# Keeping four engines in the source's order in two stages of a three-layer Trainium2 kernel, and moving one logarithm

## The chip, the cores and the metric

The kernel runs on one core of a Trainium2 chip. The core has a matrix engine (TensorE, PE in the profile; its weight loads are PEld), a vector engine (VectorE, DVE), a scalar engine for table functions (ScalarE, ACT), a general engine (GpSimd, POOL), and a queue of transfers issued by SyncE (SP). Each engine has its own stream of instructions and works it off in order; between engines, semaphores make a consumer wait for its producer. The metric is the device time of one execution in microseconds. Beside the timed runs one execution is recorded by the hardware profiler.

## What is computed

Eight images of 32 x 32 pixels with 128 channels, in 32-bit floats, pass three layers, each of which adds its result to the image.

1. *Attention*: queries, keys and values from a normalised image, four heads of 32 channels, 1024 pixels by 1024 pixels.
2. *Mixer*: each image is a sequence of 1024 tokens, worked in both directions by a state-space layer.
3. *Spectral stage*: a convolution along the sequence with fixed filters.

The heart of the mixer, cut to what matters here (c are the 16 chunks of 64 tokens):

```python
zxbcdt = x @ in_proj
z, xbc, dt = split(zxbcdt)
xbc = silu(causal_conv(xbc, conv_w) + conv_b)      # 4 taps
xh, Bm, Cm = split(xbc)
dt = softplus(dt + dt_bias);  dA = dt * A
Acs = cumsum(dA within a chunk);  xdt = xh * dt
Y_diag = einsum(Cc, Bc, exp(segsum(dA)), xdt)
states = einsum(Bc, exp(Acs_last - Acs), xdt)      # one per chunk
prev   = scan(states, exp(Acs_last))               # state before each chunk
Y_off  = einsum(Cc, prev, exp(Acs))
yg = (Y_diag + Y_off + xh * D) * silu(z)
out = (yg * rsqrt(mean(yg * yg) + eps) * norm_w) @ out_proj
```

The softplus is built of an exponential, a logarithm and a few small operations.

## The kernel before, in words

The kernel is one program in which Python functions emit instructions. A builder then fixes the order of each engine's stream. Unless it is told otherwise, it may let a later instruction go ahead of an earlier one on the same engine where the data allow it; it puts in the semaphores that the chosen order needs. Tiles come from pools with a fixed number of buffers, and a new tile in a buffer waits for the last reader of the old one.

*Attention* (about 95 to 505 us) loops over 8 images, 2 halves of the queries and 8 tiles of keys. `scores` makes the products pt (PE, L480) and their exponential pr (ACT, L485); `weigh` multiplies by the values (PE, L500) and adds two key tiles (`two`, DVE, L509); `total` sums those over the keys (PE pd, L520); `project` takes the reciprocal of the sums in small pieces (den), applies it to av, and adds the projected result to the image X. The loop is written as a pipeline: scores of step n, sums of step n-2, weights of step n-1, and a piece of `project`.

*The mixer* (about 505 to 1190 us) loops over 16 units: sequence 0 direction 0, sequence 0 direction 1, sequence 1 direction 0 and so on. A unit's iteration finishes this unit and prepares the next one, `following`. If the next unit starts a new sequence (it is then called `fresh`; this is so in each unit of direction 1 but the last), the sequence's normalised tokens are turned and its step sizes made as well. The functions and the tiles they fill, in the source's order:

- `decays`: three small products in the tile misc (PE, L794), then their exponentials rest and dec (ACT, L796 and L800)
- `turn_x`: xs is transposed (sx, PE, L810) and multiplied by the step sizes (xdt, DVE, L813)
- `turn_sums` of the unit before: two transposes of its sums of squares, in misc (PE, L1015), then a reciprocal root (rms, POOL, L1019)
- `turn_b`: sb (PE, L827), from which bk is copied (ACT, L835)
- `decayed_x`: xdd (DVE, L842), from xdt and rest, and gm
- `add_up` of the unit before: its result into X (DVE, L1026)
- `turn_tokens`, if fresh: the normalised tokens b_x are transposed (px, PE, L656)
- `between`: pl (PE, L856) from dau, and its exponential lm (ACT, L863)
- `steps`, if fresh: a generator in three pieces. The first makes pd on PE, sp_v on DVE and an exponential on ACT; the second makes sp_u, its logarithm on ACT, and sp_u again; the third makes the step sizes dt, and da.
- `chunk_states`: pst (PE, L893), from bk and xdd
- `pass_states`: the chain over the chunks, 29 dependent steps on DVE (state, L907 and L910), and four transfers on SP's queue (moved)
- `from_start`: pe (PE, L873) from dau and its exponential ec (ACT, L880)
- `spread`, for the next unit: da spread out to dau on POOL (L710)
- `project_x` and `project_z`, for the next unit: pp and pz on PE, copied or activated by ACT to xp, xs and zs
- `weigh_decays`: lm times gm (DVE, L931) and ec times ct (DVE, L935)
- `outputs`: sy (PE, L959) from xdt, lm, state, moved and ec
- `convolve` (DVE, L749), `activate_x` (ACT, L754), `project_bc` (pb, PE, L769) and `activate_bc` (bt and ct, ACT, L785) for the next unit
- `gate`, two halves: y (DVE, L974 and L982) and its square (ACT)
- `normalize`, in units of direction 0: statistics of the next sequence (b_st and b_mv on DVE, a reciprocal root ln_r on POOL)
- `project_out`: spo (PE, L989); `square_sums`: misc (PE, L1001) and its copy sums (ACT, L1009)
- `normalized`, in units of direction 0: b_shift on DVE, and b_x in eight pieces on ACT (L647)

In PSUM two buffers rotate among sx, sb, px, pl, pd, pe, pp, pz and pb, and two among pst, sy, spo and misc. [...] the exponential, the logarithm and the silu used here need loads between them (ACT_TABLE_LOAD).

Before the change the order of all engines' streams in these loops is the builder's. In the trace of before one sees, for instance, that the first four sx stand ahead of the decays on PE, that lm's product runs ahead of the chain of states, and that b_x runs between the two exponentials of lm.

## Time and profile before

| | |
|---|---|
| three runs, median (lowest, highest) | 1656.2 us (1654.26, 1657.62) |
| profiled execution | 1658.12 us |
| its span, first to last instruction | 1656.0 us |
| mean granted TensorE clock | 0.963 |
| busy, PE | 1502.1 us (91% of the span) |
| busy, DVE | 1145.9 us (69%) |
| busy, ACT | 884.4 us (53%) |
| busy, POOL | 438.8 us (26%) |
| largest groups of the two stages | exponential pr 248.1, pt 162.5, two 159.9, po 149.0, convolution 117.7, pb 114.1, state 87.3 us |

Times are in microseconds. The page divides the span in 40 slices and gives a digit for each engine and slice, its busy share in tenths. Its list of groups gives for a line, an operation and a tile the busy time, the mean of one instruction, and what ended the idle time before it. A timeline row gives the start, the length, the engine, the line, the operation, the tile written and those read, the shapes, and how many instructions the row joins (x2); in brackets stands the idle time of the engine before the row and what ended it.

### The profile page before, as it was taken

Reading aid. Unit: us, or ns where it says so; the run is one execution under the profiler, and the core shown is the slowest. Engines: PE = TensorE matmul, PEld = TensorE weight load, DVE = VectorE, ACT = ScalarE, POOL = GpSimd, SP = SyncE. Lnnn points to the kernel's source line nnn. Section 1 sums busy time; section 2 is a strip of 40 time slices with the busy share of each in tenths; the row PEclk is TensorE's granted clock in tenths of the full one; section 3 lists DMA queues with packets and bytes.
Section 4 is the critical chain, followed back from the end, with each engine's and each line's share of the span. In section 5 each row is a group of like instructions: output and inputs, shape, how many; then the busy total and the mean of one; then the engine's idle time right before and its main releaser. Section 6 shows DMA issues by size and latency. Waiting matters only on the chain. (4 is left out here: it accounts for less than half of the span.)

```text
span 1656.0 us, 45655 instructions
## 1 busy us (share of the span) xinstructions
PE 1502.1 (91%) x20118; PEld 910.7 (55%) x20118; DVE 1145.9 (69%) x2211; ACT 884.4 (53%) x1205; POOL 438.8 (26%) x504
## 2 busy tenths in 40 slices
PE   4679999999997999999999999999587899999977
PEld 3442222223223566666665666665376888888863
DVE  6856767777676787787877787878444466666745
ACT  2326666666665565656565656565154255555530
POOL 6428888500001111111112111111065401001100
PEclk9899999999997999999999999999788899999998
DMA  5002212100000000000100000000258512223238
GB/s 147 0 1 62 66 50 61 39 1 1 1 1 0 14 14 26 14 26 14 27 13 26 14 26 13 26 14 26 72 169 214 158 48 74 67 61 80 70 101 313
DMA packets 131958, 89.03 MB, mean 54 GB/s; under 512 B 41480, under 2 KB 114824, under 8 KB 131752
## 3 DMA queue, kind: packets, MB, share of 16 engines
q1 hardware_dynamic: 129640, 81.84, 17.6%
q8 instruction: 160, 2.62, 0.7%
q10 hardware_dynamic: 2112, 4.19, 0.7%
q14 instruction: 46, 0.38, 0.1%
HBM read 44.60 MB, written 33.55 MB: 47 GB/s over the span
## 5 line engine op out<-in xcount | busy, mean ns | idle before, releaser
L485 ACT ACTIVATE pr<-pt 128x1024 f32<-128x1024 f32 x256 | 248.1, 1021 | 121.6 <-PE pt L480 94.3
L509 DVE TENSOR_TENSOR two<-pr,pr 128x1024 f32<-128x1024 f32 x128 | 159.9, 1280 | 98.0 <-PE pd L520 98.0
L1260 DVE COPY gs<-pg 128x512 f32<-128x512 f32 x256 | 164.8, 686 | 85.8 <-PE pg L1249 80.7
L1262 ACT COPY gs<-pg 128x512 f32<-128x512 f32 x256 | 138.7, 595 | 147.3 <-PE pg L1249 131.4
L480 PE MATMUL pt<-q,k 32*128 32x512 f32 x1024 | 162.5, 642 | 5.2 <-DVE taps L356 3.5
L1249 PE MATMUL pg<-taps,mst 32*128 32x128 f32 x4096 | 160.7, 287 | 6.8 <-ACT gs L1262 6.8
L1249 PEld LDWEIGHTS pg<-taps,mst 32*128 32x128 f32 x4096 | 136.4, 189 | 31.6 <-issue 17.1
L500 PE MATMUL po<-pr,v 128*32 128x512 f32 x1024 | 149.0, 603 | 0.0
L1283 PE MATMUL py<-gs,u 128*32 128x128 f32 (+1 forms) x4096 | 145.2, 282 | 0.7 <-ACT gs L1262 0.4
L1283 PEld LDWEIGHTS py<-gs,u 128*32 128x32 f32 (+1 forms) x4096 | 112.6, 144 | 16.0 <-issue 0.9
L749 DVE SCALAR_TENSOR_TENSOR xs<-xp,cw,xs 128x1024 f32<-128x1024 f32 x96 | 117.7, 1293 | 2.1 <-ACT xs L741 2.1
L813 DVE TENSOR_TENSOR xdt<-sx,dt 128x1024 f32<-128x1024 f32 x32 | 37.8, 1220 | 115.2 <-PE sx L810 115.2
L769 PE MATMUL pb<-bxt,wbc 128*128 128x512 f32 x256 | 114.1, 598 | 2.0 <-issue 1.1
L480 PEld LDWEIGHTS pt<-q,k 32*128 32x128 f32 x1024 | 55.3, 184 | 102.9 <-PE pt L480 40.2
L1019 POOL TENSOR_TENSOR rms<-rms_v,mhalf 128x8 f32<-128x8 f32 x16 | 39.2, 2447 | 224.8 <-DVE rms_v L1017 224.8
L1272 POOL TENSOR_SCALAR u<-u 128x512 f32<-128x512 f32 x16 | 23.9, 1492 | 249.2 <-DMA u<-ud 235.7
L710 POOL TENSOR_TENSOR dau<-upto,da 128x2048 f32<-128x2048 f32 x16 | 57.9, 3620 | 116.0 <-PE pe L873 94.2
L520 PE MATMUL pd<-two,ones 128*32 128x512 f32 x512 | 84.8, 605 | 3.6 <-DVE two L509 2.4
L910 DVE SCALAR_TENSOR_TENSOR state<-state,dec,pst 128x64 f32<-128x64 f32 x448 | 87.3, 275 | 0.9
L769 PEld LDWEIGHTS pb<-bxt,wbc 128*128 128x128 f32 x256 | 47.2, 189 | 57.4 <-issue 54.7
L500 PEld LDWEIGHTS po<-pr,v 128*32 128x32 f32 x1024 | 28.8, 109 | 88.2 <-issue 87.9
L959 PEld LDWEIGHTS sy<-lm,xdt 64*64 64x64 f32 x2048 | 63.1, 137 | 21.1 <-issue 20.4
(279 smaller groups left out, 2920.0 us busy)
## 6 DMA issues: line engine op xcount, KB each, us to landing
ud<-sp SPq DMA_DIRECT2D x8, 1024.0 KB
u<-ud SPq DMA_DIRECT2D x32, 256.0 KB
yd<-sums SPq DMA_DIRECT2D x32, 256.0 KB
moved<-state SPq DMA_DIRECT2D x48, 128.0 KB
yt<-yd SPq DMA_DIRECT2D x6, 1024.0 KB
X<-in_x SPq DMA_DIRECT2D x8, 512.0 KB
part_p<-in_L_ffn_M_phi_plus SPq DMA_DIRECT2D x32, 128.0 KB
part_m<-in_L_ffn_M_phi_minus SPq DMA_DIRECT2D x32, 128.0 KB
```

Of the source, the lines that this page charges most:

```text
L480: nc.tensor.matmul(pt[:, i, :], lhsT=k[rows, j * P : (j + 1) * P], rhs=q[rows, cols], start=True, stop=True)
L485: nc.scalar.activation(pr[:, 2 * g : 2 * g + 2, :].rearrange("p i t -> p (i t)"), pt.rearrange("p i t -> p (i t)"), AF.Exp,)
L500: nc.tensor.matmul(po[rows, :], lhsT=vs[b][:, j, rows], rhs=pr[:, h, :], start=(j == 0), stop=(j == NT - 1))
L509: nc.vector.tensor_tensor(two, sums["pr"][:, 2 * g : 2 * g + 2, :], pr[:, 2 * g : 2 * g + 2, :], ALU.add)
L520: nc.tensor.matmul(sums["d"][(2 * g + i) * DH : (2 * g + i + 1) * DH, :], lhsT=ones[:, :DH], rhs=two[:, i, :], start=(j == 1), stop=(j == ...
L749: nc.vector.scalar_tensor_tensor(acc, xp[:, at : at + T], cw[u.d][:, n, i : i + 1], acc, ALU.mult, ALU.add)
L769: nc.tensor.matmul(u.pb[:, i * 512 : (i + 1) * 512], lhsT=wbc[u.d][:, k, :], rhs=xt[:, at : at + 512], start=(k == 0), stop=(k == KC - 1),)
L910: nc.vector.scalar_tensor_tensor(u.state[:, k, h, :], u.state[:, k - 1, h, :], u.dec[:, c, j, h : h + 1], u.pst[c][:, j, h, :], ALU.mult, ...
L1249: nc.tensor.matmul(pts[g][:, e, :], lhsT=mst[rows, n * 4 + e, :], rhs=taps[rows, cols].rearrange("p f q m i -> p (f q m i)"), start=True, ...
L1260: nc.vector.tensor_copy(to, frm)
L1262: nc.scalar.copy(to, frm)
L1283: nc.tensor.matmul(py[t * 32 : t * 32 + 32 - 16 * m, q, :], lhsT=u[:, i, m:, :, :, q * FC + f].rearrange("p k b i -> p (k b i)"), rhs=mats ...
```

## The change

Two kinds of edit are made.

- Before the attention loop, and again before the mixer's loop over units, a section is opened in which PE, DVE, ACT and POOL keep the order in which the source emits their instructions. SP's queue is not in the set. Stages outside of the two sections stay the builder's.
- In the mixer's loop the second piece of `steps` (with the logarithm) no longer follows `chunk_states`; it comes after `from_start`, where the third piece stood. The third piece (dt and da) now comes after `project_x` of the next unit, and `project_x` comes ahead of `spread`.

```diff
+IN_ORDER = {
+    mybir.EngineType.PE,
+    mybir.EngineType.DVE,
+    mybir.EngineType.Activation,
+    mybir.EngineType.Pool,
+}
...
         prs, ending = {}, iter(())
+        s.enter_context(tc.manual_schedule(engines=IN_ORDER))
         for n in range(len(units) + 2):
             if n < len(units):
                 prs[n] = scores(*units[n])
...
         activate_bc(first)
 
+        s.enter_context(tc.manual_schedule(engines=IN_ORDER))
         last = None
         misc = wide_psum(ps_s, "misc")
...
                 going = steps(following.b, following.seq)
                 next(going)
             chunk_states(u)
-            next(going, None)
             pass_states(u)
             from_start(u)
             next(going, None)
             if following:
+                project_x(following)
+                next(going, None)
                 spread(following)
-                project_x(following)
                 project_z(following)
             weigh_decays(u)
             outputs(u)
```

No arithmetic is altered.

## The prediction

> **What bounds the kernel now.** I read the page's slices first (40 of 41.4 us each), to see where TensorE is the limit.

> ```profile
> PE   4679999999997999999999999999587899999977
> DVE  6856767777676787787877787878444466666745
> ACT  2326666666665565656565656565154255555530
> ```

> The columns are time. Slices 4 to 12 are attention, 13 to 28 the mixer: TensorE stands at 9 in both but for the seam, VectorE at 6 to 8, ScalarE at 5 or 6. So both stages run at TensorE's pace, and the change costs or saves only what it adds to or takes from TensorE's idle time. The page's chain of work is cut short at a few per cent of the span and says nothing on the mixer; I read TensorE's waits there, 540 to 1160 us, instead.

> ```profile
> engine line waited for: us in total, times, longest us
> PE sy L959 <- issue: 12.6, 10, 1.5
> PE sb L827 <- DVE xdt L813: 3.4, 15, 0.2
> PE pst L893 <- DVE xdd L842: 3.2, 7, 0.5
> PE spo L989 <- DVE y L982: 3.1, 4, 1.4
> ```

> About 25 us of waits in 620: all that better order could win. Next the timeline of one unit of each kind (start, length, engine, line). Unit 4 (direction 0) starts with sx at 702.31, unit 5 (direction 1) at 740.29; 783.21 starts unit 6.

> ```profile
> 704.23 2.36 DVE L813 TENSOR_TENSOR xdt<-sx,dt 128x1024 f32<-128x1024 f32 x2 [6.52 <-PE sx L810]
> 711.52 2.58 DVE L931 TENSOR_TENSOR lm<-lm,gm 128x1024 f32<-128x1024 f32 x2
> 714.40 5.46 DVE L910 SCALAR_TENSOR_TENSOR state<-state,dec,pst 128x64 f32<-128x64 f32 x28
> 717.54 3.62 POOL L710 TENSOR_TENSOR dau<-upto,da 128x2048 f32<-128x2048 f32 x1 [8.25 <-PE pe L873]
> 719.78 3.59 DVE L935 TENSOR_TENSOR ec<-ec,ct 128x1024 f32<-128x1024 f32 x2
> 740.81 1.28 ACT L796 ACT_TABLE_LOAD   x1
> 742.11 0.20 ACT L796 ACTIVATE rest<-misc 128x32 f32<-128x32 f32 x1
> 742.20 0.38 ACT L800 ACTIVATE dec<-misc 64x32 f32<-64x32 f32 x2
> 742.88 0.38 PE L1015 MATMUL misc<-ident,sums 128*128 128x128 f32 x2
> 743.49 1.15 PE L827 MATMUL sb<-ident,bt 64*64 64x64 f32 x32 [0.23 <-DVE xdt L813]
> 747.73 2.03 ACT L647 ACTIVATE b_x<-X,b_shift,ln_r 128x128 f32<-128x128 f32 x5
> 750.90 1.23 DVE L931 TENSOR_TENSOR lm<-lm,gm 128x1024 f32<-128x1024 f32 x1 [1.32 <-ACT lm L863]
> 762.28 2.36 DVE L935 TENSOR_TENSOR ec<-ec,ct 128x1024 f32<-128x1024 f32 x2
> ```

> The reader is to see that rest and dec are ready 2.3 us into a unit, that b_x runs after them, that lm is done before the state chain, and that ec takes 3.59 us where dau overlaps it and 2.36 where not. Lengths: 37.87 to 39.53 us in direction 0 (mean 38.8), 42.3 to 42.9 in direction 1 (42.66).

> [...] dau is 3.62 us in every unit, and ec loses 1.23 us, about the overlap; the state operations, which read PSUM, keep their 0.275 us under dau. [...] The trace shows the 1.28; the next instruction starts 0.02 us later[...].

> **The change, part by part.** Standing the two programs' instructions side by side gives: equal counts on PE, DVE, POOL and SP; seven table loads fewer on ACT; attention's PE order, all of SP's, and the spectral stage unaltered. Times below are within a unit, from its start.

> *Table loads.* With the logarithm after both ec exponentials, each of seven direction-1 units saves a reload: 7 x 1.28 = 9.0 us of ACT. ACT idles some 40% of those slices, so 0 on the end. It would be up to -9 if ACT were the bound.

> *Attention.* Three small VectorE operations change places around `two` (den, two3, X). PE has 41.2 of 41.4 us busy there; slack before pd is about 0.5 us. I bound it at 0 to +3 in all and take +1.5. *Start of the mixer.* Statistics of later images, so far hoisted among its first instructions, leave: -3 to 0, I take -1.5.

> *Decays first (all units).* The three decay matmuls stood behind the first four sx and now lead. They wait for the copy of sums, which ends at 0.51: PE idles 0.5 to 0.6 us, shifting xdt by about 0.45.

> *Direction 0 (8 units).* lm's two multiplications move behind the state chain. Chain 11.85 to 17.7. POOL's dau waits only for pe of this unit, 15.1 + 0.5, so [...] lm (two SBUF inputs) can't begin until 19.3 though its inputs are old. lm 2.44 ends at 21.7, ec 2.44 at about 24. PE, after pz, is at sy at 22.7 and needs lm and the first half of ec (22.7 to 22.9): with the later half a stall of about 1.2. Sy ends near 27.7 rather than 26.2. Length 37.9 + 0.55 + 1.0 = 39.5, against 37.9 for the units without, 38.8 for the mean with the 'issue' gap in sy: +0.7 if the stall hides the gap, +2.1 if not; I take +1.4. 8 x 1.4 = +11.2 (5.6 to 16.8).

> *Direction 1 (the 7 that a fresh sequence follows).* The normalised image b_x for the next sequence used to run between lm's exponentials. It now stands, in source order, between the sums copy and this unit's table load, rest and dec. Its scale needs eight b_st, eight b_mv and a POOL power of 1.64 us, which now come after the second convolution of the unit before: shift ready about 41.5 of 39.5, so 2.05 into this unit. Eight b_x at 0.41 end at 5.4, the load at 6.7, dec at 7.2. The two transposes of the previous sums (misc) wait for dec, as they overwrite what it reads, and sb stands behind them on PE: sb at 7.6, against 3.2, PE idle 4.2 us. pl used to wait for 7.54 anyway; it comes at 11.0, so a net +3.5. The chunk states come after pl and pd, so the chain runs 18.4 to 24.2 (16.3 to 22.1 before); then sp_u, the logarithm (load 23.1 to 24.4) and da at 25.5 must pass on VectorE before lm. lm and ec take 4.9: 30.25. PE has pe, pp and pz until about 29.5; sy waits 0.7. That gives a unit of 45.8: **+3.1**. dau becomes free at da too. If lm follows da without a gap [...] dau then slips into a pause between dependent convolution steps and holds the first convolution until 37.6, the gates until 42.8, spo by 1.8: 47.7, **+5.0**, my value. The second convolution, now behind the gates, ends at 46.5 and its silu at 47.6, which the next unit's sx just tolerates. [...] 7 x 5.0 = +35 (22 to 45.5).

> *Last unit.* lm's 2.44 us now stand between the chain and sy with nothing else for PE: +2.6.

> *Sum.* 1.5 - 1.5 + 11.2 + 35 + 2.6 = +48.8 us, on the profiled execution's 1658.1 (span 1656.0, 2.1 around it). The three runs' median is 1656.2, so I forecast 1705.

> **The rivals.** *Mild* (20%): dau meets nothing in direction 1, the stalls swallow sy's issue gaps, attention gains nothing: 8 x 0.7 + 7 x 3.1 + 2.5 - 3 = +27, 1683. For it: the gaps (12.6 us) fall in sy, right after the new stall. Against: dau must run somewhere between da and the next pl, a stretch in which VectorE hardly stops.

> *Harsh* (9%): dau first in direction 1, gaps kept: 8 x 2.1 + 7 x 6.5 + 2.7 + 3 = +68, 1724. For it: GpSimd needs only da and an old pe. Against: VectorE's next instruction is issued with no semaphore to cross.

> *Faster* (8%): one mechanism, the late dec. It decides if b_x ends by about 3 us into the unit, before sb needs the transposes; that is, if the statistics, which depend on no mixer result, are ready 2.4 us sooner than my 41.5. Then the +3.5 vanish, and sy's gaps (12.6), spo's waits for y (3.1) and the seam (3) may be won: 1656.2 - 18.7 = 1637.5. Against: the eight b_st stand behind convolution and gates on VectorE, now by rule.

> *No change* (3%): PE's order is nearly the same, so PE-bound stages could stay at 1656. Against: dec's wait is in PE's own stream.

> **How the numbers follow.** My own case 60%, +30 to +68; mild 20%, harsh 9%, faster 8%, no change 3%. My case alone gives 1686 to 1724; 1668 to 1732 also takes in most of mild and harsh and leaves out the last two and some 5% of the tails. A measurement of this kernel tells 0.2% (3.3 us) from nothing: slower 0.89, same 0.03, faster 0.08.

> **What would show it.** Right: direction-1 units of 46 to 48 us with PE's sb waiting some 4 us for the transposes behind dec, b_x ahead of rest; direction-0 units near 39.5 with sy waiting 1.2 us for ec, lm after dau. Wrong: if sb still starts near 3.2, if lm runs before dau in direction 0 (a loss of 0.55 us only), or if the loss lies in attention, where I have under 3 us.

## The result and the profile after

The changed kernel takes 1707.72 us (median of four runs, 1705.17 to 1713.39) against 1656.91 us before: a ratio of 1.0311, 95% interval 1.0278 to 1.0343. Its profiled execution took 1705.17 us with a span of 1703.5, against 1656.0 before. The forecast was 1705 and slower. But the stages do not stand where the forecast put them. I cut both traces at the same instructions:

| stretch, us | before | after | difference | forecast |
|---|---|---|---|---|
| start to attention's first pt | 121.33 | 121.92 | +0.6 | 0 |
| attention, to the last product py | 382.93 | 363.06 | -19.9 | +1.5 |
| seam, to the first sx of the mixer | 31.04 | 30.14 | -0.9 | -1.5 |
| 8 units of direction 0 | 315.0 | 321.2 | +6.2 | +11.2 |
| 7 units of direction 1 with a fresh sequence | 298.6 | 361.3 | +62.7 | +35 |
| last unit, to its turned sums | 38.2 | 38.4 | +0.2 | +2.6 |
| spectral stage | 468.8 | 467.4 | -1.4 | 0 |
| span | 1656.0 | 1703.5 | +47.5 | +48.8 |

So the sum was met by two misses of opposite sign. The forecast's means for direction 0 leave out the first unit, which took 43.3 us before and 44.4 after; in both traces TensorE has half its clock there for 6.8 us.

The page's slices (40 of 42.6 us now) show both:

```profile
PE   4679999999979898988888889989757999999977
DVE  6757778777756787877777787778544366677644
ACT  2337776677746555454555555555253255555530
```

TensorE's first row of 9s, attention, ends one slice earlier, and in the mixer every second slice or more has gone from 9 to 8. The waits of TensorE in the mixer of the changed kernel (540 to 1210 us; total, times, longest):

```profile
engine line waited for: us in total, times, longest us
PE misc L1022 <- ACT dec L807: 25.3, 7, 3.8
PE sy L966 <- DVE ec L942: 15.0, 22, 0.8
PE sy L966 <- DVE lm L938: 14.8, 7, 2.1
PE misc L801 <- ACT sums L1016: 7.4, 15, 0.5
PE sy L966 <- issue: 6.6, 9, 1.3
```

Seven waits for dec, seven for lm: one each per direction-1 unit. The timeline of the changed kernel has a direction-0 unit whose sx starts at 701.53 and a direction-1 unit whose sx starts at 740.19; both follow here, engine by engine (start, length, engine, line).

```profile
715.61 3.62 POOL L717 TENSOR_TENSOR dau<-upto,da 128x2048 f32<-128x2048 f32 x1 [7.83 <-PE pe L880]
717.69 3.75 DVE L938 TENSOR_TENSOR lm<-lm,gm 128x1024 f32<-128x1024 f32 x2
740.89 3.18 ACT L654 ACTIVATE b_x<-X,b_shift,ln_r 128x128 f32<-128x128 f32 x8 [1.44 <-DVE b_shift L651]
744.08 1.28 ACT L803 ACT_TABLE_LOAD   x1
745.37 0.20 ACT L803 ACTIVATE rest<-misc 128x32 f32<-128x32 f32 x1
745.47 0.38 ACT L807 ACTIVATE dec<-misc 64x32 f32<-64x32 f32 x2
745.90 0.69 PE L1022 MATMUL misc<-ident,sums 128*128 128x128 f32 x2 [3.77 <-ACT dec L807]
746.52 1.98 PE L834 MATMUL sb<-ident,bt 64*64 64x64 f32 x32
766.16 5.78 DVE L938 TENSOR_TENSOR lm<-lm,gm 128x1024 f32<-128x1024 f32 x2
766.39 4.47 POOL L717 TENSOR_TENSOR dau<-upto,da 128x2048 f32<-128x2048 f32 x1 [16.76 <-DVE da L709]
771.87 2.35 DVE L942 TENSOR_TENSOR ec<-ec,ct 128x1024 f32<-128x1024 f32 x2
772.00 0.49 PE L966 MATMUL sy<-lm,xdt 64*64 64x64 f32 x8 [2.12 <-DVE lm L938]
```

The reader is to see three things. First, b_x, table load, rest, dec, transposes, sb: an unbroken chain, and TensorE idle for 3.77 us in it. Second, in direction 0 lm begins under dau and needs 3.75 us, where its two products took 2.4 before: the first alone takes 2.62 us instead of 1.22, with 1.54 of it under dau. Third, in direction 1: lm starts 0.23 us before dau, and yet its two products need 5.78 us. The first of them takes its usual 1.22 us and the second 4.64, 3.42 more. dau shows 4.47 us, which I read as its own 3.62 after 0.85 of waiting. By this reading dau waited for the first product of lm, ran between the two, and the second product waited for dau.

The first and the third cost more than their idle time. Windows of the changed kernel show it (PEclk is the granted share of TensorE's clock). They lie around the waits in the unit above and around the wait for dec in the next direction-1 unit, which was 3.06 us long:

```profile
core 0: us, PE busy (x) PEld busy (x) DVE busy (x) ACT busy (x) POOL busy (x), PEclk, DMA share, GB/s
746.50:750.20 3.70, 3.70 (x66) 3.56 (x66) 2.44 (x3) 0.00 (x0) 2.69 (x5) 0.50 0.02 4
838.70:840.80 2.10, 2.10 (x66) 2.02 (x66) 1.91 (x3) 0.00 (x0) 1.66 (x1) 1.00 0.03 8
741.25:744.66 3.41, 0.88 (x9) 0.65 (x6) 2.36 (x2) 3.40 (x9) 0.00 (x0) 1.00 0.00 0
768.55:771.97 3.42, 1.33 (x4) 0.25 (x2) 3.42 (x2) 3.39 (x4) 2.31 (x1) 1.00 0.00 0
771.97:778.79 6.82, 5.71 (x188) 5.33 (x190) 6.01 (x5) 1.40 (x2) 0.00 (x0) 0.50 0.01 2
833.41:836.82 3.41, 1.88 (x17) 1.64 (x16) 2.36 (x2) 3.40 (x9) 0.00 (x0) 1.00 0.00 0
836.82:840.23 3.41, 1.88 (x54) 1.72 (x56) 1.34 (x3) 1.45 (x4) 1.09 (x1) 1.00 0.02 5
```

The first two rows are sb in the two units: the same 66 instructions take 3.7 us at half the clock and 2.1 us at the full one. sb takes 3.0 to 3.7 us in six of the seven units and 2.08 in the seventh, which is also the shortest (49.7 us against 51.4 to 53.1).

The other rows show when the clock falls. In each of the fourteen traces of this case it changes only at marks 3.413 us apart. In the stretch up to the mark at 744.66 TensorE was busy for 0.88 us, and from there its clock is halved. In the one up to 771.97, ahead of sy, it was busy for 1.33 us; no wait there was longer than 2.12 us, and yet the clock is halved again, in sy. The wait of 3.06 us falls across a mark, each of the two stretches keeps 1.88 us of work, and the clock stays. In a kernel of the experiments below (da and dau late) the same unit has the same wait of 3.06 us, but most of it lies within one stretch:

```profile
830.74:834.15 3.41, 1.02 (x24) 0.86 (x26) 1.32 (x3) 2.31 (x6) 0.23 (x1) 1.00 0.00 0
834.15:837.56 3.41, 3.41 (x55) 3.29 (x51) 2.20 (x3) 0.59 (x1) 2.46 (x5) 0.50 0.02 5
```

In sy the clock is halved in all seven direction-1 units, for 3.4 or 6.8 us; before the change it is never halved in these units. TensorE's time in one of them, mean of seven, adds up so:

| us | before | after |
|---|---|---|
| waits for sums and dec (ahead of the decays and the transposes) | 0 | 4.1 |
| waits in sy (lm, ec, issue) | 0.9 | 3.6 |
| other waits | 1.2 | 0.4 |
| work of sb, px and misc | 5.1 | 6.9 |
| work of sy | 4.1 | 6.2 |
| other work | 31.5 | 30.4 |
| unit | 42.7 | 51.6 |

In attention hardly a wait is listed (2.0 us for pd before, in six waits). From 140 to 460 us TensorE counts as busy for 316.9 of 320 us before and for 320.0 after, but in these it does 888 products of pt before and 936 after:

```profile
L480 PE MATMUL pt<-q,k 32*128 32x512 f32 x888 | 139.3, 640 | 0.0
L486 PE MATMUL pt<-q,k 32*128 32x512 f32 x936 | 146.8, 640 | 0.0
```

The gain is found in the timeline of before around one product py:

```profile
414.12 0.68 DVE L540 TENSOR_TENSOR av<-av,den 128x512 f32<-128x512 f32 x1
414.72 2.35 DVE L509 TENSOR_TENSOR two<-pr,pr 128x1024 f32<-128x1024 f32 x2
416.00 1.76 PE L520 MATMUL pd<-two,ones 128*32 128x512 f32 x6
417.14 0.62 PE L500 MATMUL po<-pr,v 128*32 128x512 f32 x2
417.58 0.60 PE L520 MATMUL pd<-two,ones 128*32 128x512 f32 x2
417.60 1.44 PE L500 MATMUL po<-pr,v 128*32 128x512 f32 x6
418.97 0.38 PE L544 MATMUL py<-wout,av 128*128 128x128 f32 x1
```

and the same place in the changed kernel:

```profile
398.67 2.29 DVE L515 TENSOR_TENSOR two<-pr,pr 128x1024 f32<-128x1024 f32 x2
401.81 1.06 PE L526 MATMUL pd<-two,ones 128*32 128x512 f32 x8
402.69 1.04 PE L506 MATMUL po<-pr,v 128*32 128x512 f32 x8
403.66 0.60 PE L550 MATMUL py<-wout,av 128*128 128x128 f32 x3
```

pd and po each write bands of 32 rows. One record of them is 0.60 us long on the mean, and in the good case 8 records take 1.06 us: four start within 0.02 us and run beside each other, then the other four. Before, `two` stood behind av; its second half was ready at 417.07. pd started with the half that was there, and both pd and po fell apart into pieces. From the first pd to py it took 2.97 us instead of 1.85. In this trace a matmul that runs alone counts as just as busy as four that run together, so the loss of 1.1 us sits inside "busy". A half of an image takes 23.18 us before and 21.98 after.

### The profile page after: what moved, and what is told of

Same layout as the page of the kernel before. It is cut to its first block, busy times and chain, and to the rows that moved or that the text cites. A ratio compares the mean times of both kernels' runs of the same rounds, so it can differ in the third digit from the quotient of the medians.

```text
span 1703.5 us, 45615 instructions
## 1 busy us (share of the span) xinstructions
PE 1497.4 (88%) x20118; PEld 926.3 (54%) x20118; DVE 1181.0 (69%) x2211; ACT 874.4 (51%) x1198; POOL 446.4 (26%) x504
## 3 DMA queue, kind: packets, MB, share of 16 engines
q8 instruction: 160, 2.62, 0.7%
## 5 line engine op out<-in xcount | busy, mean ns | idle before, releaser
L506 PE MATMUL po<-pr,v 128*32 128x512 f32 x1024 | 136.7, 602 | 0.0
L756 DVE SCALAR_TENSOR_TENSOR xs<-xp,cw,xs 128x1024 f32<-128x1024 f32 x96 | 123.9, 1293 | 4.6 <-ACT xs L748 2.4
L717 POOL TENSOR_TENSOR dau<-upto,da 128x2048 f32<-128x2048 f32 x16 | 63.8, 3989 | 202.3 <-DVE da L709 125.6
L486 PEld LDWEIGHTS pt<-q,k 32*128 32x128 f32 x1024 | 55.3, 184 | 102.9 <-PE pt L486 40.2
L966 PE MATMUL sy<-lm,xdt 64*64 64x64 f32 x2048 | 81.7, 247 | 22.2 <-DVE lm L938 19.7
L966 PEld LDWEIGHTS sy<-lm,xdt 64*64 64x64 f32 x2048 | 74.8, 155 | 36.9 <-DVE lm L938 20.6
L776 PEld LDWEIGHTS pb<-bxt,wbc 128*128 128x128 f32 x256 | 47.2, 189 | 55.6 <-issue 53.8
L966 PE MATMUL sy<-ec,state 64*64 64x64 f32 x960 | 64.2, 245 | 14.0 <-DVE ec L942 11.3
```

What stands on the lines that cost most here:

```text
L486: nc.tensor.matmul(pt[:, i, :], lhsT=k[rows, j * P : (j + 1) * P], rhs=q[rows, cols], start=True, stop=True)
L506: nc.tensor.matmul(po[rows, :], lhsT=vs[b][:, j, rows], rhs=pr[:, h, :], start=(j == 0), stop=(j == NT - 1))
L756: nc.vector.scalar_tensor_tensor(acc, xp[:, at : at + T], cw[u.d][:, n, i : i + 1], acc, ALU.mult, ALU.add)
L776: nc.tensor.matmul(u.pb[:, i * 512 : (i + 1) * 512], lhsT=wbc[u.d][:, k, :], rhs=xt[:, at : at + 512], start=(k == 0), stop=(k == KC - 1),)
L966: nc.tensor.matmul(u.py[c][h * HP : (h + 1) * HP, r, j, :], lhsT=left, rhs=right, start=(kind == 0), stop=(kind == 1 or k is None),)
```

## The experiments

**Which stage, and which place in attention.** The first kernel keeps the order in attention alone: the section before the mixer's loop is left out and the moved pieces go back.

```diff
-        s.enter_context(tc.manual_schedule(engines=IN_ORDER))
         last = None
```

> The source's order is kept in attention alone; the mixer is the builder's, with its old source order. Theory (attention gained 20 us because pd no longer runs with half of its columns; the mixer lost 69 us): about 1637 us, with 21.98 us per half of an image instead of 23.18. Rival (the mixer's order also lent attention its gain, by keeping the statistics of later images out of it): about 1657 us.

Measured: 1634.54 us, ratio 0.9868 (0.985 to 0.9886), 21.98 us per half. The gain is there without the mixer's section, so it is attention's own. Of the 24 us between the two profiled executions, 18 lie in the attention loop; another 5 are in the mixer's first unit, which ran at half clock for 6.8 us before and does not here. The second kernel adds to it one exchange: the second pair of `two` in each half (key tiles 2 and 3) goes behind av again. The expectation on record calls it the fourth, by a miscount.

```diff
+            late = 1 <= n < len(units) + 1 and units[n - 1][2] == 3
+            if late:
+                next(ending, None)
             if 1 <= n < len(units) + 1:
...
-            next(ending, None)
+            if not late:
+                next(ending, None)
```

> As the kernel with only attention in the source's order, but the fourth pair of additions (two, key tiles 2 and 3 of the four pairs' second) comes behind the two reductions and the product av, as the builder had it. Theory (this one place is the whole gain): 1.2 us come back per half, 16 x 1.2 = 19, so about 1656 us. Rival (the place of den or of the addition into X made the gain): about 1637 us.

Measured: 1656.63 us, ratio 1.0 (0.9983 to 1.0018), 23.15 to 23.54 us per half: the whole gain is gone. Its timeline shows the split back:

```profile
444.82 1.76 PE L526 MATMUL pd<-two,ones 128*32 128x512 f32 x6
445.97 0.62 PE L506 MATMUL po<-pr,v 128*32 128x512 f32 x2
446.41 0.60 PE L526 MATMUL pd<-two,ones 128*32 128x512 f32 x2
```

So this one place is the gain; den and X, which the forecast also named, are not. The mixer's section alone, with attention the builder's:

> The source's order is kept in the mixer alone, with the moved pieces; attention is the builder's. Theory (the two stages' effects add up): the changed kernel plus the 21.5 us that attention gave, about 1728 us. Rival (statistics of later images, hoisted into attention or the seam, move with the mixer's section and take part of the gain along): 1718 us or less.

Measured: 1731.99 us, 1.0449 (1.0414 to 1.0483). The two stages' effects add up, to about 3 us.

**The late dec.** In the changed kernel, b_shift and b_x are emitted behind rest and dec.

```diff
             decays(u, misc)
+            if fresh:
+                normalized(following.b, following.seq)
             turn_x(u)
...
             square_sums(u, misc)
-            if u.d == 0 and u.b + 1 < B:
-                normalized(u.b + 1, seqs[u.b + 1])
```

> The changed kernel with b_shift and b_x of the next sequence emitted after rest and dec of the direction-1 unit instead of before. Theory (late dec holds the transposes and sb behind it): the wait for dec goes, 7 x 3.8 us, so about 1681 us. Rival (that wait only takes the place of another, such as pl or lm): above 1700 us.

Measured: 1676.99 us, 1.0127 (1.0107 to 1.0147): 31 us less than the changed kernel. The wait for dec has gone from the list, sb starts 2.39 us after sx and takes 2.08 us in every unit but the first, and direction-1 units take 47.2 us on the mean, not 51.6. The theory had counted the idle time alone, 27 us; the slow sb went with it.

**dau beside the products.** In the changed kernel, da and dau of the next unit go behind both products of `weigh_decays`.

```diff
             if following:
                 project_x(following)
-                next(going, None)
-                spread(following)
                 project_z(following)
             weigh_decays(u)
+            if following:
+                next(going, None)
+                spread(following)
```

> The changed kernel with dt, da and the spread dau of the next unit emitted after both products of weigh_decays, so that in direction 1 dau cannot start before lm and ec are done. Theory [...]: lm ends 4 us sooner, and of that 3 to 4.5 us per direction-1 unit is won, so 1676 to 1687 us. Rival (dau then blocks the convolution and the gates instead): 1705 to 1710 us.

Measured: 1687.54 us, 1.0179 (1.0159 to 1.0199): 20 us less, just above the range of the theory. The timeline of this kernel, a direction-1 unit:

```profile
769.71 4.53 POOL L717 TENSOR_TENSOR dau<-upto,da 128x2048 f32<-128x2048 f32 x1 [21.04 <-DVE da L709]
764.29 2.35 DVE L938 TENSOR_TENSOR lm<-lm,gm 128x1024 f32<-128x1024 f32 x2
766.56 2.35 DVE L942 TENSOR_TENSOR ec<-ec,ct 128x1024 f32<-128x1024 f32 x2
769.49 7.16 DVE L756 SCALAR_TENSOR_TENSOR xs<-xp,cw,xs 128x1024 f32<-128x1024 f32 x3
```

lm and ec take 2.35 us each, sy keeps the full clock in all seven units and has 4.1 us of work in each, not 6.2, and the bill goes to the convolution: 7.16 us for three operations that take 3.92 in the changed kernel. There dau costs less, since the gates have some slack, but spo now waits for y (5.6 us in seven waits). Both halves of the argument are seen in one kernel: the products without dau beside them, and what dau delays instead.

**Both, and the decays.** b_x behind dec, and lm's product ahead of the chain, where no dau runs:

```diff
             chunk_states(u)
+            weigh_within(u)          # lm times gm; weigh_decays keeps ec times ct
             pass_states(u)
```

> The changed kernel with two places mended: b_x behind rest and dec, and the product lm times gm ahead of the chain of states instead of behind it, where it meets no dau. Theory [...]: the waits of sy for lm go, direction 0 about 38.3 us, direction 1 about 43.5, in all about 1643 us. Rival (with lm ahead the chain of states starts later and sy waits for it instead): 1665 us or more.

Measured: 1653.88 us, 0.999 (0.9979 to 1.0). The two places are 54 of the 73 us that the mixer cost, but I had expected 10 us more. Direction 0 is at 38.7 as expected (38.3), direction 1 at 45.3 instead of 43.5. Two waits of direction 1 that the expectation did not have are listed: pl for gm, 7.4 us in seven waits, and pz for xp, 7.6 us in seven. The timeline shows the second, and ec under dau:

```profile
744.44 0.26 ACT L702 ACTIVATE sp_l<-sp_u 128x64 f32<-128x64 f32 x1 [1.15 <-DVE sp_u L700]
744.60 1.91 ACT L745 COPY xp<-pp 128x1024 f32<-128x1024 f32 x2
745.65 2.85 PE L727 MATMUL pz<-bxt,win 128*128 128x512 f32 x6 [1.08 <-ACT xp L745]
745.65 5.78 DVE L944 TENSOR_TENSOR ec<-ec,ct 128x1024 f32<-128x1024 f32 x2
```

The moved logarithm needs sp_u, which VectorE makes only after the chain. The copies of xp stand behind the logarithm on ScalarE, and pz needs their buffer. So the moved pieces, priced at nothing on ScalarE, cost 1.1 us per unit once the larger stalls are gone; and ec meets dau (5.78 us; sy waits 1.6 us per unit for it). With the first four-tile half of sx ahead of the decays besides:

> As the kernel with those two places mended, and the first four-tile half of sx emitted ahead of the three decay products. Theory (the decays' wait for the copy of sums, 0.5 us in each of 15 units, is covered again): 7 us less than that kernel, about 1636 us. Rival (the wait only moves to xdt or sb): the same time as that kernel.

Measured: 1643.76 us, 0.9922 (0.9903 to 0.9942): 10 us less by the medians, 16 by the two profiled executions (spans 1635.8 and 1652.1), of which 5 are in the first unit: it runs at half clock for 6.8 us in the one trace and not in the other. The wait for sums has gone from the list.

**The logarithm by itself.** The moved pieces under the builder's order:

> Only the moved pieces of the step sizes and of project_x in the source; all engines' order is the builder's, as before. Theory (ScalarE is not the bound, table loads are hidden): within 0.2% of 1656 us. Rival (the seven reloads are on the path): 7 x 1.28 = 9 us less, 1647 us. If the builder makes da later for it, somewhat slower than before.

Measured: 1657.43 us, 1.0 (0.9988 to 1.0012). The test does not tell what it was made for: the builder put the seven loads back, the profile counts 56 in the whole kernel, as before. The other way round, the changed kernel with the old places:

> The changed kernel (both stages in the source's order) with the logarithm, dt, da and project_x at their old places in the source, so that the seven table loads come back. Theory (loads are hidden; VectorE's chain of states starts about 1 us later behind the logarithm, da comes at about the same time, lm and ec meet dau as before): 1706 to 1713 us. Rival (the loads are on the path): 1708 + 7 x 1.28 = 1717 us or more.

Measured: 1711.29 us, 1.0315 (1.0276 to 1.0354), against 1.0311 (1.0278 to 1.0343) with the pieces moved. It has 56 loads, the changed kernel 49. In these two kernels seven loads are worth nothing that can be told from the scatter of the runs (1703 to 1713 us).

**A version faster than both kernels.** The kernel with three mended places gets a fourth: the logarithm and da ahead of the chain, so that dau runs under it.

```diff
             weigh_within(u)
+            next(going, None)
+            next(going, None)
             pass_states(u)
             from_start(u)
-            next(going, None)
             if following:
                 project_x(following)
-                next(going, None)
                 spread(following)
```

> As the kernel with three places mended, and both later pieces of the step sizes (logarithm, dt, da) emitted ahead of the chain of states, so that dau runs under the chain, which reads PSUM, and not under ec; the logarithm then stands between the exponentials again and costs two table loads more in 7 units. Theory: direction-1 units of 41 to 42 us, about 1622 us, faster than both kernels and than the one with only attention in order. Rival (the table loads, 7 x 1.28 = 9 us, and the wait of VectorE for the logarithm ahead of the chain [...]): 1636 us or more.

Measured: 1622.75 us, 0.9793 (0.977 to 0.9815). dau takes 3.62 us and ec 2.36 in direction 1, units 42.0 us against 44.7, although 7 loads are back (one per unit, not two as expected). Two waits have gone at once, sy for ec (1.6 us per unit) and pz for xp (1.1); pp now waits 0.5 us for ec, which stands behind the logarithm and a load. So this step is not dau's place alone; the logarithm's new place has a part in it. Of the 33 us by which this kernel beats the one before, 21.5 are attention's; the mixer's share is some 12. Then two smaller places:

> As the kernel with four places mended, and two more: the next sequence's statistics ahead of the convolution of the direction-0 unit with b_x behind it, so that b_x is done before the direction-1 unit starts; and gm ahead of xdd, so that pl's buffer is free sooner. Theory (pl waits 1.1 us in each of 7 units for gm and the b_x in front of bk): 7 to 8 us less, about 1615 us. Rival (the statistics delay the gates, and spo waits for y instead): 1622 us or more.

Measured: 1633.91 us, 0.9858 (0.983 to 0.9887), a miss. Direction 1 did fall to 41.2 us, but direction 0 rose to 40.2: with gm first, xdd and X came later, and the list shows pst waiting 13.9 us in eight waits for X; in three of these units the clock was halved as well. So gm first in direction 1 only:

```diff
+            if u.d == 1:
+                masked()             # gm
             u.xdd = p1.tile([P, NT, NH, HP], F32, tag="xdd", name=f"xdd{u.tag}")
...
+            if u.d == 0:
+                masked()
```

> As the kernel with two more places mended, but gm goes ahead of xdd only in direction 1. Theory (in direction 0 gm first made xdd and with it X late, and pst waits for X in the buffer it takes over, 13.9 us in 8 units): that wait goes, direction 0 back to about 38 us, direction 1 stays at 41.2, about 1616 us. Rival (the early statistics are what made direction 0 longer): 1630 us or more.

Measured: 1616.37 us, 0.9759 (0.9743 to 0.9775). Units take 37.9 and 41.1 us, against 38.8 and 42.7 before. Its waits in the mixer are small but for one kind:

```profile
PE sy L974 <- issue: 13.2, 11, 1.6
PE spo L1004 <- DVE y L989: 3.5, 1, 3.5
PE pl L869 <- DVE gm L849: 3.4, 7, 0.5
PE pp L727 <- ACT ec L893: 3.2, 7, 0.5
```

The gaps that the profile puts down to issue were not a target here, and what they are is left open.

## Why the prediction was right, and where not

- *Total and sign*: right, 1705 against 1707.7, but the closeness is luck: +27.7 us missed in direction 1 and -21.4 missed in attention nearly cancel, with smaller misses beside them. The time alone would have hidden that. Behind both misses stands one step: "the change costs or saves only what it adds to or takes from TensorE's idle time". Attention's gain lay inside the busy time, and of the 9.0 us that a direction-1 unit lost, some 3.5 us are slower work at half clock, by my estimate (1.8 in sb, px and misc, and most of 2.1 in sy).
- *Attention, +1.5*: wrong; it gained 19.9. "PE has 41.2 of 41.4 us busy there" was read as a sign that no more could be won. The listed waits (pd on two, 2.4 us in the whole stage) were the visible end of a loss of 1.2 us in 15 or 16 halves, and the forecast took the pair that moved ahead of av as a matter of slack. The exchange experiment shows that this pair is all of it.
- *Table loads, 0*: holds for the changed kernel, as far as the run with the old places can tell. What the forecast did not price is the wait for sp_u that the moved logarithm puts in front of xp; it is hidden in the changed kernel, behind lm's lateness, and 1.1 us per unit without it.
- *Decays first, 0.5 to 0.6 us*: as forecast, 7.4 us in 15 waits of at most 0.5.
- *Direction 0, 39.5 us*: 39.55 measured on the mean of seven units, against 38.8 before. The path is as described (dau before lm, lm late, sy waiting for ec), but the number was hit by luck. That lm can't begin under dau was my estimate (in the trace of before, ec loses 1.23 us there); by its record lm begins there and takes 1.40 us longer. 39.5 was worked out for units without an issue gap in sy; those took 38.65, 0.8 more than before and not 1.6. The wait for ec is 0.7 us per unit, not 1.2, and pst, pe and pz together took 0.6 us less. The forecast's lower end, +0.7, assumed that the stall hides the issue gaps; they stayed at 0.7 us per unit.
- *Direction 1, +5.0*: +9.0 measured. The late dec is as forecast in kind: b_x ended at 3.9 us into the unit shown, not 5.4, and sb came at 6.3, not 7.6, with TensorE idle for 3.8 us and not 4.2. What was put at nothing is the clock: sb, px and misc then had 1.8 us more of work. The other step that failed is "dau then slips into a pause between dependent convolution steps". lm did come first, by 0.23 us, but only with one product. dau, by then waiting, ran before the second, and 3.4 us fell on lm and ec, where TensorE waits, and not 1.9 on the spo behind the convolution. sy waited 3.5 us for lm and ec instead of 0.7, and ran at half clock for a part of the time: its work took 6.2 us and not 4.1. The pauses alone make little of that; in the kernel with two places mended, sy has such pauses at the full clock and 4.3 us of work. The rival 'harsh' came nearest, with +6.5.
- *The waits for dec and sums*: the forecast says that the transposes overwrite what dec reads. In the kernel's text they fill columns 512 to 767 of misc, while the decays fill 768 to 863 and the copy of sums reads 0 to 255. So these waits, 32.7 us together, come with the shared tile and not with the data, as far as the text shows. No run gave the three a tile each; whether the waits can be dropped that way is open.
- *Last unit, +2.6*: 0.2 measured. pst and pe, no longer interleaved with pl, ended about 1.2 us earlier and the chain with them (16.32 us into the unit instead of 17.48). So sy began only 1.5 us later, and it took 7.5 us instead of 8.7; why it was shorter was not traced.
- *The rival 'faster'* hung on dec alone. With dec mended the kernel was still 1.3% slower, so that rival's mechanism was not sufficient. The way to a faster mixer took lm and ec out of dau's way too.

## What to carry to other kernels

A busy share near 100% does not mean that TensorE is at its limit. Where several narrow matmuls can run beside each other, compare the time of one group in two places of the trace before calling a stage bound; a late operand for half of the group hides in "busy" (here 2.97 us instead of 1.85, where TensorE counts as busy for 316.9 of 320 us). Price a stall by more than its idle time: from the second unit to the fifteenth, a stretch of 3.413 us with less than 1.48 us of TensorE's work at the full clock had half the clock behind it, and there sb took up to 3.7 us instead of 2.1. An order written by hand must be checked engine by engine for what stands in front of short operations that others wait for (here b_x before dec, and the logarithm before xp). In these kernels dau on GpSimd and VectorE's products of two SBUF tiles held each other up (5.78 us for a pair instead of 2.36), while the state operations, which also read PSUM, kept their 0.275 us under dau: look for work of the second kind to put a long GpSimd operation under, and keep it away from work that TensorE is waiting for.

## What was not expected of the hardware

- At the edge the place of the marks 3.413 us apart decided on the clock: the same wait of 3.06 us in the same unit left sb at 2.08 us in one kernel and made it 3.17 in another. And no long wait was needed: behind a stretch with 1.33 us of work and no pause above 2.12 us the clock was halved as well.
- Two VectorE products that stand back to back did not keep dau out: recorded from 0.23 us after the first began, it ran between them, as I read the lengths (4.47 us for dau with its 0.85 us of waiting; 1.22 and 4.64 us for the products, 5.78 for the pair instead of 2.36). The waiting engine came next, although VectorE had its second product ready.
- One late `two` cost TensorE 1.1 us per half of an image while its recorded idle time there was at most 0.5 us (2.97 us for pd and po instead of 1.85).
